# Attention and two quantised convolutions: phases of equal length on TensorE, and what is moved around them

## The chip, the cores and the metric

The kernel runs on one core of one Trainium2 chip. The metric is device time in microseconds (us), the median over executions. Engines are named as in the profile: PE (TensorE matmul), PEld (its weight loads), DVE (VectorE), ACT (ScalarE), POOL (GpSimd) and SP (SyncE, here a queue of DMAs).

## The reference, cut to what matters

```python
# layer 0, x: (4, 128, 64, 64); 4 heads of 32 channels, 4096 positions per image
x_norm = group_norm(x)                       # 8 groups of 16 channels
q, k, v = split(qkv_w @ x_norm + qkv_b)      # each to (b, head, position, 32)
attn = softmax(q @ k.T * 32**-0.5)           # 4096 x 4096 for each image and head
x = x + proj_w @ (attn @ v) + proj_b
# layer 1
out = relu(batchnorm(conv3x3(x, lsq_quantize(w1, alpha1))))
out = batchnorm(conv3x3(out, lsq_quantize(w2, alpha2)))
return relu(out + x)
```

`lsq_quantize` rounds w / alpha to 3 bits. The batch norms take their statistics over all four images, so no image can finish layer 1 alone.

## The kernel before, in words

**Tiles.** An image has 4096 positions: 8 chunks of 512 for queries (`qb`, 0 to 7), 32 tiles of 128 for keys (`kt`, 0 to 31). A block is one image and one `qb`; there are 32, numbered `n`. A step is one block and one `kt`: 1024 steps. The scores of a step are two pairs of heads. For each pair `scores` (L425) issues four matmuls into one of three PSUM tiles `s`, and ACT (L427) writes the exponentials into half of a tile `p` (128 x 4 heads x 512, 1 MB). There are eight such tiles, in `ppool`; the first two to be handed out are the halves of image 0's x, which stay until its last projection. `weights` (L438) multiplies all four heads of `p` with v into `acc`, 512 columns a head; an f32 matmul appears as two instructions in the trace. Scores run in row groups of 64 (64*128 in the trace), products with v and projections in column groups of 32 (128*32).

**Sums of the softmax.** DVE adds each `p` to `r` (L450, first of them L448). For the steps in `MOVED` (six of 32) POOL issues a DMA instead that adds `p` to `rm` (L445, first L443), and in the next block `merge` (L471) adds `rm` to `r`. A `p` is free when the product and the add, or the move, are done.

**Order.** It is written out by hand. PE runs phases: three pairs of scores, the product of one step, three pairs, the products of two steps, and so on:

```python
for s, w in ((3, 1), (3, 2)):
    run_scores(s)
    run_weights(w)
```

After each product `side` runs what `schedule` has listed for that `kt`. Matmuls beside the attention are put at `slots`, the ends of the one-step phases. A "visit" is a projection in two column halves (L301: "pk", "pq", "pv" for k, q, v of a chunk; L467: "l", the row sums) followed, a step later, by its evacuation: for k and q an ACT activation (L335) and a DVE instruction (L336), then a POOL DMA to DRAM (`kd`, `qd`); for v a DVE add (L355); for the sums an ACT copy `ls` (L475). A visit's two halves go to one place or to two. Visits share two PSUM banks (`psa`) with `acc`. Block n + 1 also finishes block n: the sums, their inversion by way of DRAM (`spread`, `invert`, `gather`), `weigh` on DVE (L514, "av"), `project` (L301, "po") and `store` (L524, L525 "y"). `acc` is copied by ACT (L460, "av") at a block's end.

**Image to image.** While image b runs, image b + 1's norm (`norm_parts`, with POOL, DVE and three small matmul groups) and projections are visited. Image 0 projects some chunks before the loop and the others in blocks 0 and 1, with x from the pinned halves. In the last image DVE quantises both weights piece by piece (`taps`, L174 to L191) into `wq`. SP issues all loads in order: x (L230), k (L394), v (L398), q (L405).

**After attention.** Two convolutions in bands of 16 rows (`load_band` L558, `split_band` L549 and L550, 36 matmuls each half at L722), each with batch statistics and a copy into `cv`. `mid` is an SBUF pool that opens where the attention's pools have closed.

Of the kernel before, what the change touches and what calls it, by code (L numbers as in the profile page):

```python
# [16 lines left out]
F32 = mybir.dt.float32  # L17
# [61 lines left out]
def _fast_body(ctx, tc, x, norm_w, norm_b, qkv_wt, qkv_b, proj_wt, proj_b,  # L79
# [56 lines left out]

    wq = [const.tile([P, TAPS, P], F32R, name=f"wq{i}") for i in range(2)]
    alpha_s = []  # L140
    gfac = 1.0 / math.sqrt(float(P * P * TAPS) * QP)

    def quant_tasks(pool):

        tasks = []
        for i, (w, alpha) in enumerate(((w1, alpha1), (w2, alpha2))):
# [20 lines left out]
            for c in range(3):  # L167


                def taps(i=i, c=c, w=w, t=t):  # L170
                    tk, tq = (pool.tile([P, 2, FB], F32, name=f"t{n}{i}{c}", tag=n) for n in "kq")
                    wr, q0, qh, ql = (u[:, e, : 3 * P].rearrange("p (t o) -> p t o", o=P)
                                      for u in (tk, tq) for e in range(2))
                    nc.sync.dma_start(out=wr, in_=w[:, 3 * c : 3 * c + 3, :])  # L174
                    yield
                    nc.vector.tensor_scalar(q0, wr, t["inv"], -8.0, ALU.mult, ALU.max)
                    nc.vector.tensor_scalar(q0, q0, 8.0, None, ALU.min)
                    nc.vector.tensor_scalar(qh, q0, SPLIT, None, ALU.add)
                    yield
                    nc.vector.tensor_scalar(qh, qh, SPLIT, None, ALU.subtract)  # L180
                    nc.vector.tensor_tensor(ql, q0, qh, ALU.subtract)
                    nc.vector.scalar_tensor_tensor(wr, qh, t["a_h"], wr, ALU.mult, ALU.subtract)
                    yield
                    nc.vector.scalar_tensor_tensor(wr, qh, t["a_l"], wr, ALU.mult, ALU.add)
                    nc.vector.scalar_tensor_tensor(wr, ql, t["a_h"], wr, ALU.mult, ALU.add)
                    nc.vector.scalar_tensor_tensor(wr, ql, t["a_l"], wr, ALU.mult, ALU.add)
                    yield
                    nc.vector.scalar_tensor_tensor(q0, wr, t["ninv"], q0, ALU.mult, ALU.add)
                    nc.vector.tensor_scalar(q0, q0, QN, QP, ALU.max, ALU.min)
                    nc.vector.tensor_scalar(q0, q0, ROUND, None, ALU.add)  # L190
                    nc.vector.tensor_scalar(wq[i][:, 3 * c : 3 * c + 3, :], q0, ROUND, None,  # L191
                                            ALU.subtract)

                tasks.append(taps)
        return tasks
# [3 lines left out]

    dram = ctx.enter_context(tc.tile_pool(name="dram", bufs=1, space=bass.MemoryType.DRAM))
    kpool = ctx.enter_context(tc.tile_pool(name="kpool", bufs=NB + 1))
    pss = ctx.enter_context(tc.tile_pool(name="pss", bufs=3, space=PSUM))
    psa = ctx.enter_context(tc.tile_pool(name="psa", bufs=2, space=PSUM))
# [5 lines left out]
    qpool = att.enter_context(tc.tile_pool(name="qpool", bufs=2))  # L211
    stage = att.enter_context(tc.tile_pool(name="stage", bufs=1))
    xpool = att.enter_context(tc.tile_pool(name="xpool", bufs=3))
    ppool = att.enter_context(tc.tile_pool(name="ppool", bufs=8))
    rpool = att.enter_context(tc.tile_pool(name="rpool", bufs=1))
    sums = att.enter_context(tc.tile_pool(name="sums", bufs=2))
    wpool = att.enter_context(tc.tile_pool(name="wpool", bufs=1))
# [189 lines left out]

    blocks = [(b, qb) for b in range(B) for qb in range(NB)]
    pts, acc, rsum, msum = {}, {}, {}, {}
    MOVED = (4, 9, 14, 19, 24, 28)  # L410


    def scores(pair):
# [14 lines left out]

    def weights(step):
        n, kt = divmod(step, NK)
        v = vs[blocks[n][0], kt // KB]
        pt = pts[step]
        if kt == 0:
            acc[n] = psa.tile([P, FB], F32, name=f"acc{n}", tag="a")
        for h in range(HEADS):
            nc.tensor.matmul(acc[n][h * D : (h + 1) * D, :], v[:, kt % KB, h * D : (h + 1) * D],  # L438
                             pt[:, h, :], start=(kt == 0), stop=(kt == NK - 1))
        if kt in MOVED:  # L440
            if kt == MOVED[0]:
                msum[n] = rpool.tile([P, HEADS, FB], F32, name=f"rm{n}", tag="rm")
                nc.gpsimd.dma_start(out=msum[n], in_=pt)  # L443
            else:
                nc.gpsimd.dma_start(out=msum[n], in_=pt, accum_op=ALU.add)  # L445
# [132 lines left out]
        load_k(b, j)  # L578
        load_v(b, j)

    for what, j in (("k", 0), ("q", 0), ("k", 1), ("v", 0), ("k", 2), ("v", 1), ("k", 3), ("v", 2)):
        for f in first_chunk(j, what, True):
            f()
        if what == "v":
            load_k(0, j + 1)


# [3 lines left out]
    def fetch(b, j):  # L591
        xin[b, j] = load_x(b, j)

    def schedule(n, before):
        b, qb = blocks[n]
        todo = []
        slots = [kt for kt in range(NK - 1) if (n * NK + kt) % 3 == 0]
        two = b + 1 < B and qb in (2, 3)
        full = two or n == 1

        def add(kt, f):
            todo.append((kt, f))

        def visit(kts, first, second, evacuate=None):
            add(kts[0], first)
            add(kts[-1], second)
            if evacuate:
                add(kts[-1] + 1, evacuate)

        if before:  # L610
            add(1, before["merge"])
            kts = slots[3:4] if full else slots[3:5]
            visit(kts, lambda: before["sums"](0), lambda: before["sums"](1))
            kt = kts[-1]
            add(kt + 1, before["spread"])
            add(kt + 3, before["invert"])
            add(kt + 4, before["gather"])
            add(kt + 6, before["residual"])
            add(slots[9] - 2, before["weigh"])
            add(slots[9], before["project"])  # L620
            add(slots[9] + 1, before["store"])
        if n + 1 < len(blocks):
            add(14, lambda: load_q(*blocks[n + 1]))
        if n == 0:
            for kt, what, j in ((0, "k", 4), (2, "q", 1), (3, "v", 3), (6, "k", 5), (9, "k", 6),
                                (12, "v", 4), (15, "k", 7), (18, "v", 5), (21, "v", 6),
                                (24, "v", 7)):
                visit((kt,), *first_chunk(j, what, False))
                if what == "k":
                    add(kt + 2, lambda j=j: load_k(0, j))  # L630
        if n == 1:
            for i, j in zip((0, 1, 2, 4, 5, 6), range(2, NB)):
                visit(slots[i : i + 1], *first_chunk(j, "q", False))
        if b + 1 < B:
            if qb == 1:
# [4 lines left out]
                late[b] = norm_parts(b + 1, st)  # L640
                add(15, late[b][0])
                for i in (0, 1):
                    add(slots[7 + i], late[b][1 + 2 * i])
                    add(slots[7 + i] + 1, late[b][2 + 2 * i])
            if qb == 2:
                add(slots[0], late[b][5])
                add(slots[0] + 1, late[b][6])
            chunks = {1: (), 2: (0, 1), 3: (2, 3), 4: (4,), 5: (5,), 6: (6,), 7: (7,)}
            for i, j in enumerate(chunks.get(qb, ())):
                p = project_parts(b + 1, j, lambda j=j: xin[b + 1, j])  # L650
                if not two:
                    places = dict(k=slots[0:2], q=slots[5:7], v=slots[7:9])
                elif i == 0:
                    places = dict(k=slots[1:2], q=slots[2:3], v=slots[4:5])
                else:
                    places = dict(k=slots[5:6], q=slots[6:7], v=slots[7:9])
                    add(8, lambda j=j: fetch(b + 1, j))
                for what, kts in places.items():
                    visit(kts, *p[what])
            if qb > 0 and qb + 1 in chunks:  # L660
# [15 lines left out]

    pieces = (piece for task in quant_tasks(stage) for piece in task())
    steps = len(blocks) * NK
    at = {"pair": 0, "step": 0}
    todo, parts = [], {}  # L680

    def side(kt):
        while todo and todo[0][0] <= kt:
            todo.pop(0)[1]()

    def run_scores(count):
# [2 lines left out]
            at["pair"] += 1  # L689

    def run_weights(count):
        for _ in range(min(count, steps - at["step"])):
            n, kt = divmod(at["step"], NK)
            if kt == 0:
                assert not todo
                todo[:] = schedule(n, parts.get(n - 1))
            weights(at["step"])
            at["step"] += 1
            if kt == NK - 2:
                parts[n] = finish_parts(n)  # L700
            if kt == NK - 1:
                parts[n]["copy"]()
            else:
                side(kt)

    run_scores(2)
    while at["step"] < steps:
        for s, w in ((3, 1), (3, 2)):
            run_scores(s)
            run_weights(w)  # L710

# [30 lines left out]

    mid = ctx.enter_context(tc.tile_pool(name="mid", bufs=1))
    cv = [mid.tile([P, N], F32, name=f"cv{b}") for b in range(B)]

    def batch_norm(i, st):

# [38 lines left out]
    def first(m):  # L788
        if m == 5:
            count_bad()  # L790
        if m + 3 < len(bandlist):
            load_band(*bandlist[m + 3])
        if m + 2 < len(bandlist) and m > 0:
# [512 lines left out]
```

## Time and profile before

| | |
|---|---|
| median of 3 executions | 2590.27 us (2589.32 to 2590.64) |
| the profiled execution, its time | 2589.98 us |
| the profiled execution, its span | 2588.2 us |
| granted PE clock | 0.992 |
| attention loop in the trace | about 29 to 2266 us |
| convolutions | about 2266 us to the end |

The span is from the first to the last instruction in the trace. A row of a group gives its busy time and the mean length of one instruction, then the engine's idle time before the group and what ended most of it. A row of the timeline gives the start, the length, the engine and line, and how many like instructions are merged (x12 at L425 is three pairs of scores).

### The profile page before, as it was taken

Reading aid. Unit: us, or ns where it says so; the run is one execution under the profiler, and the core shown is the slowest. Engines: PE = TensorE matmul, PEld = TensorE weight load, DVE = VectorE, ACT = ScalarE, POOL = GpSimd, SP = SyncE. Lnnn points to the kernel's source line nnn. Section 1 sums busy time; section 2 is a strip of 40 time slices with the busy share of each in tenths; the row PEclk is TensorE's granted clock in tenths of the full one; section 3 lists DMA queues with packets and bytes.
Section 4 is the critical chain, followed back from the end, with each engine's and each line's share of the span. In section 5 each row is a group of like instructions: output and inputs, shape, how many; then the busy total and the mean of one; then the engine's idle time right before and its main releaser. Section 6 shows DMA issues by size and latency. Waiting matters only on the chain.

```text
span 2588.2 us, 48399 instructions
## 1 busy us (share of the span) xinstructions
PE 2517.2 (97%) x20394; PEld 1223.4 (47%) x20394; DVE 2140.3 (83%) x1402; ACT 2081.9 (80%) x2275; POOL 281.4 (11%) x456
## 2 busy tenths in 40 slices
PE   6999999999999999999999999999999999999894
PEld 3444444444444444444444444444444444477773
DVE  5898888888988898888988988888999998953344
ACT  4888899999988999999988899999889898911223
POOL 2111111111011111110011111110000000100000
PEclk9999999999999999999999999999999999999997
DMA  5876766698667767697667666986655757634004
GB/s 160 191 187 172 177 161 149 154 206 201 162 148 178 178 155 171 149 225 171 160 171 161 164 159 150 207 202 142 151 130 126 154 126 148 146 80 145 1 1 164
DMA packets 147417, 400.04 MB, mean 155 GB/s; under 512 B 59240, under 2 KB 60008, under 8 KB 118648
## 3 DMA queue, kind: packets, MB, share of 16 engines
q0 software_dynamic: 45888, 280.59, 47.9%
q1 hardware_dynamic: 100728, 115.23, 16.8%
q8 instruction: 162, 2.65, 0.4%
q10 hardware_dynamic: 576, 1.05, 0.1%
q14 instruction: 63, 0.52, 0.1%
HBM read 105.32 MB, written 55.83 MB: 62 GB/s over the span
## 4 chain that ended last, share of the span: by engine, by line
PE 88%; DVE 5%; issue 3%; DMA 2%; ACT 1%; POOL 0%; SPq 0%; DVEq 0%; POOLq 0%; ACTq 0%
PE s L425 39%; PE acc L438 34%; PE c L722 9%; DVE r L450 3%; DMA rm<-p 2%; PE l L467 1%; PE po L301 1%; PE pk L301 1%; PE pq L301 1%; PE pv L301 1%; ACT p L427 1%; DVE res L844 1%; DMA xh<-in_x_dram 0%; DMA q<-qst 0%; DVE st L570 0%
## 5 line engine op out<-in xcount | busy, mean ns | idle before, releaser
L427 ACT ACTIVATE p<-s 128x1024 f32<-128x1024 f32 x2048 | 1940.2, 1034 | 235.0 <-PE s L425 158.7
L450 DVE TENSOR_TENSOR r<-r,p 128x2048 f32<-128x2048 f32 x768 | 1758.4, 2290 | 97.3 <-ACT p L427 48.1
L425 PE MATMUL s<-q,k 64*128 64x512 f32 x8192 | 1162.3, 413 | 3.9 <-ACT p L427 2.2
L438 PE MATMUL acc<-p,v 128*32 128x512 f32 x8192 | 1021.1, 601 | 0.6 <-DVE v L355 0.6
L425 PEld LDWEIGHTS s<-q,k 64*128 64x128 f32 x8192 | 711.7, 185 | 631.9 <-issue 298.0
L438 PEld LDWEIGHTS acc<-p,v 128*32 128x32 f32 x8192 | 198.6, 109 | 453.7 <-issue 446.3
L445 POOL DMA_DIRECT2D rm<-p x160 | 138.6, 866 | 950.7 <-ACT p L427 783.6
L775 ACT COPY cv<-c 128x512 f32<-128x512 f32 x64 | 37.6, 587 | 220.8 <-DVE st L774 220.8
L722 PE MATMUL c<-hi,wq 128*128 128x512 f32 x576 | 150.1, 405 | 8.3 <-DVE hi L805 6.8
L722 PE MATMUL c<-lo,wq 128*128 128x512 f32 x576 | 148.1, 402 | 0.0
L774 DVE BATCH_NORM_STATS2 st<-c 128x6 f32<-128x512 f32 x64 | 44.7, 699 | 124.5 <-PE c L722 102.5
L722 PEld LDWEIGHTS c<-hi,wq 128*128 128x128 f32 x576 | 109.4, 191 | 40.1 <-issue 8.9
L722 PEld LDWEIGHTS c<-lo,wq 128*128 128x128 f32 x576 | 109.0, 189 | 28.9
L448 DVE TENSOR_TENSOR r<-p,p 128x2048 f32<-128x2048 f32 x32 | 73.3, 2291 | 25.0 <-ACT p L427 25.0
L336 DVE SCALAR_TENSOR_TENSOR kst<-pk,b,kst 128x512 fp32r<-128x512 f32 x32 | 24.0, 751 | 73.2 <-ACT kst L335 73.2
L336 DVE SCALAR_TENSOR_TENSOR qst<-pq,b,qst 128x512 fp32r<-128x512 f32 x32 | 24.0, 750 | 41.6 <-ACT qst L335 41.6
L471 POOL DMA_DIRECT2D r<-rm x31 | 26.3, 848 | 159.8 <-PE s L425 91.9
L340 POOL DMA_DIRECT2D qd<-qst x31 | 23.3, 753 | 177.6 <-DVE qst L336 130.2
L443 POOL DMA_DIRECT2D rm<-p x32 | 17.8, 556 | 223.3 <-ACT p L427 136.4
L335 ACT ACTIVATE kst<-pk,b 128x512 fp32r<-128x512 f32 x32 | 22.4, 701 | 21.7 <-PE pk L301 21.7
L340 POOL DMA_DIRECT2D kd<-kst x28 | 20.6, 734 | 167.6 <-DVE kst L336 159.6
L467 PE MATMUL l<-r,ones 128*32 128x256 f32 (+1 forms) x504 | 37.9, 383 | 0.5 <-issue 0.5
(129 smaller groups left out, 672.0 us busy)
## 6 DMA issues: line engine op xcount, KB each, us to landing
rm<-p POOLq DMA_DIRECT2D x192, 1024.0 KB, 7.9
q<-qd SPq DMA_DIRECT2D x248, 128.0 KB
r<-rm POOLq DMA_DIRECT2D x31, 1024.0 KB, 7.1
x<-in_x_dram SPq DMA_DIRECT2D x80, 256.0 KB
k<-kd SPq DMA_DIRECT2D x124, 128.0 KB
qd<-qst POOLq DMA_DIRECT2D x31, 512.0 KB, 6.9
kd<-kst POOLq DMA_DIRECT2D x28, 512.0 KB, 4.0
y<-x POOLq DMA_DIRECT2D x32, 256.0 KB, 5.0
```

The costliest lines, as they stand in the source:

```text
L301: nc.tensor.matmul(out[cs, :], w[:, cs], x, start=True, stop=True)
L336: nc.vector.scalar_tensor_tensor(lo, ps[what], bias, t[:, 0, :], ALU.add, ALU.subtract)
L340: (nc.sync if start else nc.gpsimd).dma_start(out=dst[b, j].rearrange("s p n -> p s n"), in_=t)
L425: nc.tensor.matmul(s[:, i, :], k[r, half, c0 : c0 + P], q[r, half, part, :], start=(part == 0), stop=(part == 1))
L427: nc.scalar.activation(pts[step][:, 2 * half : 2 * half + 2, :], s, AF.Exp, scale=SCALE)
L438: nc.tensor.matmul(acc[n][h * D : (h + 1) * D, :], v[:, kt % KB, h * D : (h + 1) * D], pt[:, h, :], start=(kt == 0), stop=(kt == NK - 1))
L445: nc.gpsimd.dma_start(out=msum[n], in_=pt, accum_op=ALU.add)
L448: nc.vector.tensor_tensor(rsum[n], pts[step - 1], pt, ALU.add)
L450: nc.vector.tensor_tensor(rsum[n], rsum[n], pt, ALU.add)
L467: nc.tensor.matmul(t["l"][h * D : (h + 1) * D, cs], ones, r[:, h, cs], start=first, stop=end)
L722: nc.tensor.matmul(ps[:, j, :].rearrange("p (r w) -> p r w", w=W), w[:, tap, :], part[:, j * RB + kh : j * RB + kh + RB, kw : kw + W], sta ...
L774: nc.vector.bn_stats(st[:, b * NB + c, :], ps[:, j, :])
```

## The change

It rewrites the order in the attention loop and moves a few buffers:

- The product of a step is cut into two halves of 256 columns. PE alternates three pairs of scores with three halves, and the loop begins with three pairs in place of two. Visits stand at the last half of such a phase (`ends`), and `schedule` counts in halves; the places of the visits are new.
- `ppool` has nine tiles in place of eight. In the last image's blocks 1 to 6 seven steps in place of six are moved by DMA.
- The second convolution's weights are quantised into a tile that POOL stores to DRAM (`wqd`). After attention SP loads them (`raw_w`), and DVE copies them into `wq[1]` in the first convolution.
- The second image's norm and projections come one block later. Of image 0, v's chunk 3 is projected before the loop, q's chunk 1 later in block 0, and q's chunks 2 to 7 in block 1 take x from DRAM again.

```diff
-    ppool = att.enter_context(tc.tile_pool(name="ppool", bufs=8))
+    ppool = att.enter_context(tc.tile_pool(name="ppool", bufs=9))
...
+    MOVED, MOVED_LAST = (4, 9, 14, 19, 24, 28), (3, 7, 11, 15, 19, 23, 27)
...
-    def weights(step):
+    def weights(step, half):
...
+        cs = slice(half * FB // 2, (half + 1) * FB // 2)
         for h in range(HEADS):
-            nc.tensor.matmul(acc[n][h * D : (h + 1) * D, :], v[:, kt % KB, h * D : (h + 1) * D],
-                             pt[:, h, :], start=(kt == 0), stop=(kt == NK - 1))
+            nc.tensor.matmul(acc[n][h * D : (h + 1) * D, cs], v[:, kt % KB, h * D : (h + 1) * D],
+                             pt[:, h, cs], start=(kt == 0 and half == 0),
+                             stop=(kt == NK - 1 and half == 1))
+        if half == 0:
+            return
...
-        slots = [kt for kt in range(NK - 1) if (n * NK + kt) % 3 == 0]
-        two = b + 1 < B and qb in (2, 3)
+        ends = [p for p in range(2 * NK - 2) if (2 * n * NK + p) % 3 == 2]
+        two = b + 1 < B and qb in ((3, 4, 5) if b == 0 else (2, 3))
...
+        def visit(i, first, second, evacuate=None, split=True):
+            at_half(ends[i], first)
+            e = ends[i + 1 if split else i]
+            at_half(e, second)
             if evacuate:
-                add(kts[-1] + 1, evacuate)
+                at_half(e + 1, evacuate)
...
+            e = visit(5 if two else 4 if n == 1 else 6, lambda: before["sums"](0), lambda: before["sums"](1),
+                      split=not two and n != 1)
...
+            at_half(ends[18] - 4, before["weigh"])
+            at_half(ends[18], before["project"])
+            at_half(ends[18] + 2, before["store"])
         if n + 1 < len(blocks):
-            add(14, lambda: load_q(*blocks[n + 1]))
+            add(24 if n == 0 else 14, lambda: load_q(*blocks[n + 1]))
         if n == 0:
...
+            for i, what, j in ((0, "k", 4), (2, "k", 5), (4, "v", 4), (6, "k", 6), (8, "v", 5),
+                               (10, "k", 7), (12, "q", 1), (14, "v", 6), (16, "v", 7)):
+                visit(i, *first_chunk(j, what, False), split=False)
...
         if n == 1:
...
+            for i, j in zip((0, 2, 8, 10, 12, 14), range(2, NB)):
+                if j > 3:
+                    at_half(ends[i - 3], lambda j=j: fetch(0, j))
+                visit(i, *project_parts(0, j, lambda j=j: xin[0, j])["q"], split=False)
...
                 if not two:
-                    places = dict(k=slots[0:2], q=slots[5:7], v=slots[7:9])
...
+                    for what, i in dict(k=1, q=10, v=13).items():
+                        visit(i, *p[what])
+                    continue
+                for what, e in (dict(k=2, q=7, v=9) if i == 0 else dict(k=11, q=13, v=15)).items():
+                    visit(e, *p[what], split=False)
...
-    run_scores(2)
-    while at["step"] < steps:
-        for s, w in ((3, 1), (3, 2)):
-            run_scores(s)
-            run_weights(w)
+    run_scores(3)
+    while at["half"] < 2 * steps:
+        run_scores(3)
+        run_weights(3)
...
+    raw_w = mid.tile([P, TAPS, P], F32, name="raw_w")
+    wq.append(mid.tile([P, TAPS, P], F32R, name="wq1"))
+    nc.sync.dma_start(out=raw_w, in_=wqd)
...
+        if m == 6:
+            nc.vector.tensor_copy(wq[1], raw_w)
```

More of the change, by code (lines that the diff above doesn't have):

```diff
@@ L135, in rsqrt_eps @@
         return r
-    wq = [const.tile([P, TAPS, P], F32R, name=f"wq{i}") for i in range(2)]
+    dram = ctx.enter_context(tc.tile_pool(name="dram", bufs=1, space=bass.MemoryType.DRAM))
+    wq = [const.tile([P, TAPS, P], F32R, name="wq0")]
+    wqd = dram.tile([P, TAPS, P], F32, name="wqd")
     alpha_s = []
@@ L190, in taps @@
                     nc.vector.tensor_scalar(q0, q0, ROUND, None, ALU.add)
-                    nc.vector.tensor_scalar(wq[i][:, 3 * c : 3 * c + 3, :], q0, ROUND, None,
-                                            ALU.subtract)
+                    cs = slice(3 * c, 3 * c + 3)
+                    if i == 0:
+                        nc.vector.tensor_scalar(wq[0][:, cs, :], q0, ROUND, None, ALU.subtract)
+                    else:
+                        nc.vector.tensor_scalar(ql, q0, ROUND, None, ALU.subtract)
+                        nc.gpsimd.dma_start(out=wqd[:, cs, :], in_=ql)
                 tasks.append(taps)
         return tasks
-    dram = ctx.enter_context(tc.tile_pool(name="dram", bufs=1, space=bass.MemoryType.DRAM))
     kpool = ctx.enter_context(tc.tile_pool(name="kpool", bufs=NB + 1))
@@ L409, in _fast_body, with moved @@
     pts, acc, rsum, msum = {}, {}, {}, {}
-    MOVED = (4, 9, 14, 19, 24, 28)
+    MOVED, MOVED_LAST = (4, 9, 14, 19, 24, 28), (3, 7, 11, 15, 19, 23, 27)
+    def moved(n):
+        b, qb = blocks[n]
+        return MOVED_LAST if b == B - 1 and 0 < qb < NB - 1 else MOVED
     def scores(pair):
@@ L434, in weights @@
         pt = pts[step]
-        if kt == 0:
+        if kt == 0 and half == 0:
             acc[n] = psa.tile([P, FB], F32, name=f"acc{n}", tag="a")
+        cs = slice(half * FB // 2, (half + 1) * FB // 2)
         for h in range(HEADS):
-            nc.tensor.matmul(acc[n][h * D : (h + 1) * D, :], v[:, kt % KB, h * D : (h + 1) * D],
-                             pt[:, h, :], start=(kt == 0), stop=(kt == NK - 1))
-        if kt in MOVED:
-            if kt == MOVED[0]:
+            nc.tensor.matmul(acc[n][h * D : (h + 1) * D, cs], v[:, kt % KB, h * D : (h + 1) * D],
[3 more added lines that the diff above has]
+            return
+        if kt in moved(n):
+            if kt == moved(n)[0]:
                 msum[n] = rpool.tile([P, HEADS, FB], F32, name=f"rm{n}", tag="rm")
@@ L579, in load_kv @@
         load_v(b, j)
-    for what, j in (("k", 0), ("q", 0), ("k", 1), ("v", 0), ("k", 2), ("v", 1), ("k", 3), ("v", 2)):
+    for what, j in (("k", 0), ("q", 0), ("k", 1), ("v", 0), ("k", 2), ("v", 1), ("k", 3), ("v", 2),
+                    ("v", 3)):
         for f in first_chunk(j, what, True):
             f()
-        if what == "v":
+        if what == "v" and j < 3:
             load_k(0, j + 1)
@@ L596, in schedule, with at_half @@
         todo = []
-        slots = [kt for kt in range(NK - 1) if (n * NK + kt) % 3 == 0]
-        two = b + 1 < B and qb in (2, 3)
-        full = two or n == 1
+        ends = [p for p in range(2 * NK - 2) if (2 * n * NK + p) % 3 == 2]
+        two = b + 1 < B and qb in ((3, 4, 5) if b == 0 else (2, 3))
+        def at_half(p, f):
+            todo.append((p, f))
         def add(kt, f):
[L602 to L606, printed above, removed]
+            todo.append((2 * kt + 1, f))
@@ L607, in visit @@
+        def visit(i, first, second, evacuate=None, split=True):
+            at_half(ends[i], first)
+            e = ends[i + 1 if split else i]
+            at_half(e, second)
             if evacuate:
-                add(kts[-1] + 1, evacuate)
+                at_half(e + 1, evacuate)
+            return e
         if before:
             add(1, before["merge"])
-            kts = slots[3:4] if full else slots[3:5]
-            visit(kts, lambda: before["sums"](0), lambda: before["sums"](1))
@@ L614, in schedule @@
[L614 to L621, printed above, removed]
+            e = visit(5 if two else 4 if n == 1 else 6, lambda: before["sums"](0), lambda: before["sums"](1),
+                      split=not two and n != 1)
@@ L622, in schedule @@
+            at_half(e + 2, before["spread"])
+            at_half(e + 6, before["invert"])
+            at_half(e + 8, before["gather"])
+            at_half(e + 12, before["residual"])
+            at_half(ends[18] - 4, before["weigh"])
+            at_half(ends[18], before["project"])
+            at_half(ends[18] + 2, before["store"])
         if n + 1 < len(blocks):
-            add(14, lambda: load_q(*blocks[n + 1]))
+            add(24 if n == 0 else 14, lambda: load_q(*blocks[n + 1]))
         if n == 0:
[L625 to L628, printed above, removed]
+            for i, what, j in ((0, "k", 4), (2, "k", 5), (4, "v", 4), (6, "k", 6), (8, "v", 5),
+                               (10, "k", 7), (12, "q", 1), (14, "v", 6), (16, "v", 7)):
+                visit(i, *first_chunk(j, what, False), split=False)
@@ L629, in schedule @@
                 if what == "k":
-                    add(kt + 2, lambda j=j: load_k(0, j))
+                    at_half(ends[i] + 5, lambda j=j: load_k(0, j))
+        if n == 0:
+            for j in (2, 3):
+                add(25 + j, lambda j=j: fetch(0, j))
         if n == 1:
-            for i, j in zip((0, 1, 2, 4, 5, 6), range(2, NB)):
-                visit(slots[i : i + 1], *first_chunk(j, "q", False))
+            for i, j in zip((0, 2, 8, 10, 12, 14), range(2, NB)):
+                if j > 3:
+                    at_half(ends[i - 3], lambda j=j: fetch(0, j))
+                visit(i, *project_parts(0, j, lambda j=j: xin[0, j])["q"], split=False)
@@ L634, in schedule @@
+        qn = qb if b else qb - 1
         if b + 1 < B:
-            if qb == 1:
+            if qn == 1:
                 st = small.tile([P, NB, 6], F32, name=f"st{b + 1}", tag="st")
@@ L642, in schedule @@
                 for i in (0, 1):
[L643 to L648, printed above, removed]
+                    at_half(ends[13 + 2 * i], late[b][1 + 2 * i])
+                    at_half(ends[13 + 2 * i] + 3, late[b][2 + 2 * i])
+            if qn == 2:
+                at_half(ends[0], late[b][5])
+                at_half(ends[0] + 1, late[b][6])
+            if b == 0:
+                chunks = {2: (), 3: (0, 1), 4: (2, 3), 5: (4, 5), 6: (6,), 7: (7,)}
+            else:
+                chunks = {1: (), 2: (0, 1), 3: (2, 3), 4: (4,), 5: (5,), 6: (6,), 7: (7,)}
             for i, j in enumerate(chunks.get(qb, ())):
@@ L651, in schedule @@
                 if not two:
-                    places = dict(k=slots[0:2], q=slots[5:7], v=slots[7:9])
[L653 to L656, printed above, removed]
+                    for what, i in dict(k=1, q=10, v=13).items():
[3 more added lines that the diff above has]
+                    visit(e, *p[what], split=False)
+                if i == 1:
                     add(8, lambda j=j: fetch(b + 1, j))
-                for what, kts in places.items():
-                    visit(kts, *p[what])
-            if qb > 0 and qb + 1 in chunks:
+            if qn > 0 and qb + 1 in chunks:
                 add(22, lambda j=chunks[qb + 1][0]: fetch(b + 1, j))
@@ L678, in _fast_body, with side @@
     steps = len(blocks) * NK
-    at = {"pair": 0, "step": 0}
+    at = {"pair": 0, "half": 0}
     todo, parts = [], {}
-    def side(kt):
-        while todo and todo[0][0] <= kt:
+    def side(p):
+        while todo and todo[0][0] <= p:
             todo.pop(0)[1]()
@@ L691, in run_weights @@
     def run_weights(count):
-        for _ in range(min(count, steps - at["step"])):
-            n, kt = divmod(at["step"], NK)
-            if kt == 0:
+        for _ in range(min(count, 2 * steps - at["half"])):
+            n, p = divmod(at["half"], 2 * NK)
+            if p == 0:
                 assert not todo
                 todo[:] = schedule(n, parts.get(n - 1))
-            weights(at["step"])
-            at["step"] += 1
-            if kt == NK - 2:
+            weights(*divmod(at["half"], 2))
+            at["half"] += 1
+            if p == 2 * NK - 3:
                 parts[n] = finish_parts(n)
-            if kt == NK - 1:
+            if p == 2 * NK - 1:
                 parts[n]["copy"]()
             else:
-                side(kt)
-    run_scores(2)
-    while at["step"] < steps:
-        for s, w in ((3, 1), (3, 2)):
-            run_scores(s)
-            run_weights(w)
+                side(p)
+    run_scores(3)
+    while at["half"] < 2 * steps:
+        run_scores(3)
+        run_weights(3)
     bandlist = [(b, g) for b in range(B) for g in range(H // BR)]
```

## The prediction

> **What bounds the kernel now.** I began with the page: busy shares, the span in slices, the costliest groups.
>
> ```profile
> PE 2517.2 (97%) x20394; PEld 1223.4 (47%) x20394; DVE 2140.3 (83%) x1402; ACT 2081.9 (80%) x2275; POOL 281.4 (11%) x456
> ...
> L427 ACT ACTIVATE p<-s 128x1024 f32<-128x1024 f32 x2048 | 1940.2, 1034 | 235.0 <-PE s L425 158.7
> L450 DVE TENSOR_TENSOR r<-r,p 128x2048 f32<-128x2048 f32 x768 | 1758.4, 2290 | 97.3 <-ACT p L427 48.1
> L425 PE MATMUL s<-q,k 64*128 64x512 f32 x8192 | 1162.3, 413 | 3.9 <-ACT p L427 2.2
> L438 PE MATMUL acc<-p,v 128*32 128x512 f32 x8192 | 1021.1, 601 | 0.6 <-DVE v L355 0.6
> ```
>
> TensorE (PE) is the bound: 97%, with almost no idle time put down to its two large groups. But a group's busy time also holds waits between its own matmuls, so I read PE's timeline, where the distance from one start to the next is the true price. Around 260 us (columns: start, length, engine, line), and then ACT beside it:
>
> ```profile
> 260.02 1.66 PE L425 MATMUL s<-q,k 64*128 64x512 f32 x12
> 261.61 1.07 PE L438 MATMUL acc<-p,v 128*32 128x512 f32 x8
> 262.61 1.89 PE L425 MATMUL s<-q,k 64*128 64x512 f32 x12
> 264.43 1.92 PE L438 MATMUL acc<-p,v 128*32 128x512 f32 x16
> 266.28 1.67 PE L425 MATMUL s<-q,k 64*128 64x512 f32 x12
> 267.88 1.07 PE L438 MATMUL acc<-p,v 128*32 128x512 f32 x8
> 268.76 1.05 PE L301 MATMUL pk<-x,wn 128*32 128x256 f32 x16
> ```
>
> ```profile
> 260.16 0.59 ACT L460 COPY av<-acc 128x512 f32<-128x512 f32 x1
> 260.85 5.61 ACT L427 ACTIVATE p<-s 128x1024 f32<-128x1024 f32 x6
> ```
>
> Three pairs of scores take 1.59 to 1.60 us (260.02 to 261.61), a product with v for one step 1.00 (261.61 to 262.61), for two steps 1.85. The short phase is thus 2.60 us, the long one 3.45. ACT needs 2.86 for three exponentials (half of 5.61, plus a seam). After a short phase with nothing beside it the next scores find the third PSUM buffer still full: 262.61 to 264.43 is 1.82, not 1.60. Over the whole timeline of PE, 683 score phases, I count some 118 of these, of 0.15 to 0.25 us: **20.6 us** hidden in "busy". The larger stops, read the same way: 5.5 at 37 to 50 us (a projection waits for its PSUM bank, 1.7 and 2.6, then scores 1.3), 3.4 at 85 to 175 (the largest, 1.8, is ACT waiting for a buffer that a move "rm<-p" holds), 5.9 at 1917 to 2057 (a projection waits for DVE's "av").
>
> [...] the product of one step takes 0.88 when a 128*32 projection follows (267.88 to 268.76), 1.00 when 64*128 scores do, so 0.12 a switch. [...]
>
> **The change, part by part.**
>
> 1. *Halves and equal phases.* Each step's 4 products of 512 columns become 8 of 256; phases become 3 pairs and 3 halves. The number of phases, hence of switches, stays at 683. Is the split free? No row has p times v at 256 columns. The nearest rows, same weights of 32 columns: a projection of two 256-column halves ("pk" x16) takes 0.98 before scores, "po" with 512 columns x8 takes 0.97, "pv" with four times 128 columns x32 takes 0.98. So below 0.01 per split. From above: 0.03 per split, the most by which a first group exceeds a following one (0.88 against 1.85-1.00=0.85), times 1024 is +31. [...] I take 0. Three halves: 1.85-0.85/2=1.425, so a phase of 1.60+1.42=**3.02 us** against ACT's 2.86: the short-phase stalls go, **-20.6**.
>
> 2. *What is late next: ACT's copies.* A copy of 0.59 to 0.70 ("av", "ls", "kst", "qst") comes behind three exponentials, begun 0.76 after a phase's start. They end at 3.62, the copy at 4.21 to 4.32, while the next exponential could start at 3.02+0.76=3.78: late by 0.43 to 0.54. A 2.60 phase with no delay costs 0.16, so the next stall is 0.16+(2.60-3.02)+0.43 or 0.54 = 0.17 or 0.28 if the delayed phase has no visit; with half a visit (0.43) it is nil. From the new places: k is exposed in 17 blocks (0.28), the sums in 23 (0.17), "av" in a third of 31 (0.17); q's delay meets v's visit. Sum 4.8+3.9+1.8=**+10.5**. If every one of about 112 copies stalled, it would be 25 to 31.
>
> 3. *Opening.* Visits of block 0 stand two phases apart, so the 5.5 goes. v's chunk 3 moves ahead of the loop (0.87), where scores wait for "q<-qst" to 31.92 in any case: its 0.98 in the loop is saved. **-6.5**. k 4 to 7 keep their POOL and SP issues, some earlier or later; "load_q" goes from step 14 to 24. Its own wait for "qd" (landing 4.3, POOL queue before it) and eight SP issues end some 5 us before block 1 needs it, by about 11 steps of 2.1 us less 20. Taken as 0; up to +5 if not.
>
> 4. *Nine buffers, x from DRAM, the norm later.* Six more loads of 256 KB on SP, in a stretch where the 16 DMA engines are 75% busy; the two pinned x buffers come free after block 0. Of the 3.4 I take **-2.5**.
>
> 5. *Seventh move in six blocks.* Six adds fewer, 6x2.29=13.7 us of DVE, which is 93% busy there (519.87 of 560 us). DVE is not the bound, only late at two projections: half of 5.9, **-3**. Moves then stand four steps apart, about 8.5 us, against 7.4 to land; POOL's queue behind them holds "y" and the merge, with slack of a block.
>
> 6. *Second weights.* Three POOL stores of 192 KB, in blocks with DMA at 65%: 0. At the end SP issues "raw_w" (590 KB) before band 3. At the 231 GB/s seen there, 2.6 us, less than one band's 8.6 us of convolution: between 0 and 3, taken **+1**. The DVE copy costs about 0.76 (the cast of 1188 columns) where DVE is 39% busy: 0.
>
> Unknown collisions in the rewritten order: **+2**. Sum: -20.6+10.5-6.5-2.5-3+1+2 = **-19** on a span of 2588.2. That execution took 2589.98, 0.3 below the median 2590.27, so about **2571**.
>
> **Rivals.**
>
> *A. The halves cost.* Each extra group of four costs 0.03 [...]: +31 on 2571 is 2602. For it: PEld's loads double and the first group after a switch is dearer. Against: the pk/po/pv rows. It decides from 19/1024=0.019 us per split: there the gain is gone. Chance 0.15.
>
> *B. ACT's copies take it back.* All 112 stall at 0.28: +31 instead of +10.5, so 2592 less what visits cover, about 2588. For it: ACT is 90% busy in mid-attention. Against: visits cover q and v by their places. Chance 0.14.
>
> *C. The phases equalise nothing,* since the third half waits for the current phase's first exponential. It ends about 0.76+0.95=1.7 after the start and is wanted at 1.60+0.85=2.45, 0.7 later, so unlikely: only parts 3 to 5 stay, 2590-12+3=2581. Chance 0.13.
>
> Forecast: 0.58, its own range 2558 to 2583.
>
> **How the numbers follow.** C and the forecast are faster, with a little of B: 0.73. B is mostly within 0.2%, about what a measurement of this kernel can tell: 0.10. A and the bad end of B: 0.17. For 8 in 10 the range runs from 2556 (no new stall at all) to 2600 (the split at 0.028 us).
>
> **What would show it.** In the new timeline three halves before scores at 1.42 to 1.44 us: right; 1.50 or more: A. Score phases of 1.60 after phases without a visit, and of 1.77 to 1.88 only behind a copy: step 2; a whole comb of them: B. ACT's idle time grows by a few us only. The stops at 37 to 50 us and at 173 gone, those near 1917 and 2055 halved. A first stop at block 1 ended by "q<-qd" would refute step 3. I am wrong if the time is above 2585.

## The result, and the profile after

The changed kernel takes 2589.36 us at the median, the kernel before 2590.53 in the same comparison: ratio 0.9995, interval 0.9983 to 1.0008. That is no change that can be measured; forecast were 2571 us. The profiled execution has a span of 2587.8 us against 2588.2. So the question is where 19 us of expected gain went. One execution of c_hold (below) took 5305.06 us, twice the others, and is left out of its ratio.

The page after, rows that answer to those of before:

```profile
PE 2504.4 (97%) x28586; PEld 1491.1 (58%) x28586; DVE 2125.1 (82%) x1397; ACT 2086.2 (81%) x2275; POOL 288.8 (11%) x465
...
L436 PE MATMUL s<-q,k 64*128 64x512 f32 x8192 | 1143.7, 410 | 9.8 <-ACT p L438 7.9
L450 PE MATMUL acc<-p,v 128*32 128x256 f32 x16384 | 1026.7, 383 | 1.0 <-DVE v L361 1.0
```

The scores are 18.6 us shorter in busy time (1162.3 before), the products 5.6 longer (1021.1), and PE as a whole 12.8 shorter, yet the span is the same. A busy time holds short waits too (in the kernel before, the row of scores at 262.61 us is 1.89 long, its neighbours 1.66 and 1.67), so the rows alone do not say where the time went. PE's timeline shows the equal phases as intended (start, length, engine, line, operation, count):

```profile
1006.32 1.50 PE L450 MATMUL acc<-p,v 128*32 128x256 f32 x24
1007.76 1.66 PE L436 MATMUL s<-q,k 64*128 64x512 f32 x12
1009.35 1.50 PE L450 MATMUL acc<-p,v 128*32 128x256 f32 x24
1010.78 1.66 PE L436 MATMUL s<-q,k 64*128 64x512 f32 x12
```

Three halves 1.43 us, three pairs 1.59: 3.02 a phase. I went through PE's whole timeline of both kernels, took the undisturbed length from every row and added up the rest; the choice of that length shifts such a sum by about 1 us. The comb of small stops (up to 0.3 us) fell from 21.6 to **1.4 us**. The larger stops rose from 20.9 to **34.8 us**:

| larger stops, us | before | after |
|---|---|---|
| opening, to 60 us | 8.7 | 3.4 |
| rest of blocks 0 and 1, to 230 us | 3.4 | 7.4 |
| 230 to 1700 us | 1.0 | 5.4 |
| last image, to 2260 us | 6.6 | 18.6 |
| tail | 1.2 | 0 |

The balance is -20.2 +13.9 = -6.3 us. Some 3 to 7 us go into the products (below); one or two stay unexplained. Three of the stops, as they look. First the end of block 7 at 607 us, a row of ACT, then one of PE:

```profile
608.33 1.94 ACT L438 ACTIVATE p<-s 128x1024 f32<-128x1024 f32 x2 [2.24 <-DMA rm<-p]
```

```profile
609.40 0.73 PE L436 MATMUL s<-q,k 64*128 64x512 f32 x4 [1.36 <-ACT p L438]
```

The bracket is the idle time and what ended it. ACT wants a tile p, a move still holds it, and PE is left without a free score bank. Second the largest stop, at 1907 us in the last image, in four views: SP's queue before and after, then DVE and PE after.

```profile
1851.65 5.11 SPq L405 DMA_DIRECT2D q<-qd  x8
...
1896.95 0.35 SPq L174 DMA_DIRECT2D tk<-in_L_conv_w_dram  x1
```

```profile
1887.97 12.94 SPq L411 DMA_DIRECT2D q<-qd  x8
...
1901.81 0.35 SPq L177 DMA_DIRECT2D tk<-in_L_conv_w_dram  x1
```

```profile
1910.56 0.42 DVE L179 TENSOR_SCALAR tk<-tk,inv 128x384 f32<-128x384 f32 x1 [10.62 <-DMA tk<-in_L_conv_w_dram]
```

```profile
1917.02 1.93 PE L307 MATMUL po<-av,wp 128*32 128x512 f32 x8 [8.70 <-DVE av L529]
```

Before, q's loads were out long before the weights' piece `tk`, and DVE began on that piece at 1906.43 without a wait. After, SP issues it only behind q's eight loads; DVE stands 10.6 us before it with its adds and "av" queued behind; PE waits for "av". Third, in block 1, the sums wait for the merge of rm into r (shown with d_open).

### The profile page after: what moved, and what is told of

Its sections match the earlier page's. It is cut to its first block, busy times and chain, and to the rows that moved or that the text cites. A ratio compares the mean times of both kernels' runs of the same rounds, so it can differ in the third digit from the quotient of the medians.

```text
span 2587.8 us, 64784 instructions
## 1 busy us (share of the span) xinstructions
PE 2504.4 (97%) x28586; PEld 1491.1 (58%) x28586; DVE 2125.1 (82%) x1397; ACT 2086.2 (81%) x2275; POOL 288.8 (11%) x465
## 4 chain that ended last, share of the span: by engine, by line
PE 87%; DMA 7%; issue 3%; DVE 2%; ACT 1%; POOL 0%; SPq 0%; POOLq 0%; ACTq 0%; DVEq 0%
PE s L436 38%; PE acc L450 34%; PE c L749 10%; DMA rm<-p 4%; PE po L307 1%; PE l L482 1%; PE pk L307 1%; PE pv L307 1%; PE pq L307 1%; ACT p L438 1%; DMA q<-qd 1%; DVE r L465 1%; DVE res L876 1%; DMA x<-in_x_dram 0%; DMA r<-rm 0%
## 5 line engine op out<-in xcount | busy, mean ns | idle before, releaser
L436 PE MATMUL s<-q,k 64*128 64x512 f32 x8192 | 1143.7, 410 | 9.8 <-ACT p L438 7.9
L450 PE MATMUL acc<-p,v 128*32 128x256 f32 x16384 | 1026.7, 383 | 1.0 <-DVE v L361 1.0
L450 PEld LDWEIGHTS acc<-p,v 128*32 128x32 f32 x16384 | 462.9, 109 | 486.0 <-issue 248.6
L460 POOL DMA_DIRECT2D rm<-p x166 | 144.3, 869 | 874.8 <-ACT p L438 522.8
L307 PE MATMUL po<-av,wp 128*32 128x512 f32 x256 | 35.2, 622 | 9.1 <-DVE av L529 9.1
L341 ACT ACTIVATE kst<-pk,b 128x512 fp32r<-128x512 f32 x32 | 22.4, 701 | 21.6 <-PE pk L307 21.6
```

The lines of the kernel that those rows point to most:

```text
L307: nc.tensor.matmul(out[cs, :], w[:, cs], x, start=True, stop=True)
L436: nc.tensor.matmul(s[:, i, :], k[r, half, c0 : c0 + P], q[r, half, part, :], start=(part == 0), stop=(part == 1))
L450: nc.tensor.matmul(acc[n][h * D : (h + 1) * D, cs], v[:, kt % KB, h * D : (h + 1) * D], pt[:, h, cs], start=(kt == 0 and half == 0), stop= ...
```

## The experiments

Each ratio is to the kernel before on the same chip, with its 95% interval. The runs named a_ (but a_uneven) and b_split share one chip, those named c_ and a_uneven a second, those named d_ a third, so runs of two groups are compared through their ratios. Line numbers of the same statement differ a little from run to run, since an edit adds lines.

### Is it the split?

b_split is the kernel before, with

```diff
-        for h in range(HEADS):
+        for half, h in ((i, h) for i in range(2) for h in range(HEADS)):
+            cs = slice(half * FB // 2, (half + 1) * FB // 2)
...
```

and with the matmuls' output and p cut to the columns `cs`.

> The kernel before with each step's product issued as two halves of 256 columns, one right after the other, and nothing else changed (phases stay one step and two steps). The phase lengths of the two traces (2.85 us for three steps in the kernel before, 2 x 1.43 in the changed one; with a visit 2.73 against 2.75) say 0.01 to 0.02 us for each three splits, 341 of these: +3 to +7 us, 2593 to 2597 us. Rival S, that the split eats the whole comb of 20 us: 2608 to 2612 us.

Measured: 1.0006 (0.9997 to 1.0015), 2593.88 us against 2592.24. The split costs 0 to 4 us, not 20: rival S falls. Its trace says the same by another way: a product of two steps takes 1.86 us (from 1003.29 to 1005.15) against 1.85 (from 1001.99 to 1003.84 in the kernel before), 0.01 for two steps or some 5 us over 1024.

### The equal phases undone

a_uneven is the changed kernel with

```diff
-        run_scores(3)
-        run_weights(3)
+        for w in (2, 4):
+            run_scores(3)
+            run_weights(w)
```

and the visits at those phases' ends.

> The changed kernel with phases of two and four halves in turn, as before, instead of three and three (places of visits at the ends of these phases). Undoes the equal phases alone. If the comb of 0.15 to 0.25 us stops is due to the short phase, it is back: some 230 of the 341 short phases have no visit, +35 us at 0.16, less what the longer ones give back to moves and DVE: 2605 to 2625 us. Rival: the comb's saving was never real time, because PE would have waited elsewhere; then 2588 to 2593 us, with less waiting for moves.

Measured: 1.0135 (1.0118 to 1.0152), 2624.73 us, at the upper end of what the comb said. Its timeline of PE has the long score phase (1.76) behind the short product:

```profile
1002.73 1.07 PE L450 MATMUL acc<-p,v 128*32 128x256 f32 x16
1003.73 1.83 PE L436 MATMUL s<-q,k 64*128 64x512 f32 x12
1005.49 1.93 PE L450 MATMUL acc<-p,v 128*32 128x256 f32 x32
```

So the equal phases are worth their time in this order of visits; the rest of the change took it back.

### Seven moves, and q's place in SP's queue

a_moves6:

```diff
-    MOVED, MOVED_LAST = (4, 9, 14, 19, 24, 28), (3, 7, 11, 15, 19, 23, 27)
+    MOVED, MOVED_LAST = (4, 9, 14, 19, 24, 28), (4, 9, 14, 19, 24, 28)
```

> The changed kernel with six moved steps in place of seven in blocks 1 to 6 of the last image. Theory M (moves): the seventh move puts the moves 4 steps, about 8.5 us, apart while one takes 7.6 us at the median and up to 13.8 to land; so POOL waits for the move before, p tiles stay held, ACT waits for them and PE stops at about 1984, 2137 and 2187 us. Then these three go (about 5 us), POOL's waits of rm for rm in the last image fall from 161 us towards the 44 of the kernel before, and the time is 2581 to 2585 us. Theory Q (order on SP): the last image's largest stop, 8.9 us at 1907 us, comes from weights that SP loads late behind q, and moves matter little: 2588 to 2590 us. Rival S (the split costs what the comb gave): 2588 to 2590 us.

Measured: 0.9978 (0.9968 to 0.9988), some 4 us under the changed kernel's 0.9995, whose interval it just meets. Between 1700 and 2260 us a move on POOL waits for the move before it (rm for rm) 46.8 us in 7 waits, against 148.0 in 18; the 161 of the expectation has two waits of the merge in it. The stop at 1984 us shrinks from 2.4 to 0.8, those at 2137 and 2187 are gone. PE in the changed kernel, then in a_moves6:

```profile
2187.41 1.19 PE L436 MATMUL s<-q,k 64*128 64x512 f32 x8
2190.49 0.73 PE L436 MATMUL s<-q,k 64*128 64x512 f32 x4 [1.89 <-ACT p L438]
```

```profile
2186.97 1.66 PE L436 MATMUL s<-q,k 64*128 64x512 f32 x12
```

Theory M holds for these three stops. But DVE has its seventh add back, and PE now waits 3.7 us for "av" at 2050, so that the last image's larger stops fall only from 18.6 to some 17 us in the trace. By the times, the add that the seventh move saved was worth less than the tile that it held.

a_loadq, and a_both with both edits:

```diff
-            add(24 if n == 0 else 14, lambda: load_q(*blocks[n + 1]))
+            add(24 if n == 0 else 14 if n == 1 else 2, lambda: load_q(*blocks[n + 1]))
```

> The changed kernel with the load of the next block's q listed at step 2 instead of step 14 from block 2 on, so that SP issues it before the spread and the gather of the sums and not behind them. Theory Q: the quantised weights' load is issued at once, DVE no longer waits 10.6 us for it, the stop of 8.9 us at 1907 us and its two after-effects (0.9 and 0.75 us) go: 2578 to 2581 us. Theory M: the stop stays, since p tiles are held by the moves: 2588 to 2590 us. Rival S: no change.

> The changed kernel with both edits: six moved steps everywhere and q's load at step 2. If M and Q are both right and add up, 10 + 5 us: 2572 to 2576 us. If only Q is right 2578 to 2581, if only M 2581 to 2585; rival S 2588 to 2590 us.

Measured: a_loadq 0.9997 (0.9983 to 1.001), a_both 0.9981 (0.9972 to 0.999): no gain of its own, and both forecasts missed. The trace of a_loadq (2598.68 us, one of its slowest executions, against a median of 2592.9) has lost the 8.9 us at 1907, but has new stops at block starts, 3.3 at 1176, 3.2 at 1734 and 5.0 at 2038 us. That of a_both (2585.51 us) has lost it too, and has 3.1 each at 1172 and 1731. My reading, which these runs do not test by themselves, is that q's 1 MB now lands where the moves are late. As a test of Q by time they were inconclusive, since they mend one lateness in the place of another. I then asked why moves are late at all where there are only six.

### Stores ahead of moves in POOL's queue

POOL's queue at the same block's end, before and after:

```profile
579.92 0.85 POOL L445 DMA_DIRECT2D rm<-p  x1 [9.49 <-ACT p L427]
587.75 0.75 POOL L340 DMA_DIRECT2D qd<-qst  x1 [6.98 <-DMA rm<-p]
591.04 0.86 POOL L445 DMA_DIRECT2D rm<-p  x1 [2.53 <-ACT p L427]
600.67 0.58 POOL L359 DMA_DIRECT2D vd<-vst  x1 [8.77 <-DVE vst L355]
602.93 0.83 POOL L445 DMA_DIRECT2D rm<-p  x1 [1.68 <-ACT p L427]
```

```profile
580.63 0.75 POOL L346 DMA_DIRECT2D qd<-qst  x1 [9.70 <-DVE qst L342]
581.37 0.91 POOL L460 DMA_DIRECT2D rm<-p  x1
588.22 0.58 POOL L365 DMA_DIRECT2D vd<-vst  x1 [5.94 <-DVE vst L361]
596.34 0.84 POOL L460 DMA_DIRECT2D rm<-p  x1 [7.55 <-DMA rm<-p]
608.74 0.83 POOL L460 DMA_DIRECT2D rm<-p  x1 [11.55 <-issue]
```

Before, a move waits for ACT's p and goes; the store of q comes behind it, and the one store ahead of a move, v's at 600.67, is done before that move's p is. After, the visits of q and v end a little earlier in the block, their stores stand ahead of the moves of steps 19 and 24, and POOL waits there for DVE. The first store is issued after a wait of 9.70 us, and "rm<-p" at 581.37 goes out only 0.7 us behind it, though it had no need of that store and the move before it had landed at 578.8 (570.09 and 8.7 us). The moves then run into each other until the block ends: this one lands only at 595.82, after 14.4 us, the next, issued at 596.34, at 608.22, and with that ACT has its tile (the stop at 607 above).

c_hold, on top of a_moves6, keeps the stores in a list that is emptied behind the next move:

```diff
+            elif b > 0:
+                held.append(lambda: nc.gpsimd.dma_start(out=dst[b, j].rearrange("s p n -> p s n"), in_=t))
...
+            while held:
+                held.pop(0)()
```

> Six moves everywhere, as in a_moves6 (0.9978 of the kernel before), and each store of a next image's k, q or v ("kd", "qd", "vd") is issued on POOL behind the next move instead of at its evacuation. Theory P (order on POOL): in the changed kernel the visits of q and v end a little before steps 19 and 24, so POOL's queue has their stores, which wait for DVE, ahead of the moves of those steps; the moves slip, those of steps 24 and 28 meet the loads of the next image's k and v at a block's end, and ACT waits for p tiles there. Then the stops near 607, 618, 1165 and 1725 us go, some 5 to 6 us: ratio about 0.9957, 2580 us on a chip where the kernel before takes 2591. Rival D (DVE is what is late, the moves only suffer from it): no change from a_moves6, 0.9978.

Measured: **0.9957** (0.9941 to 0.9973), the number expected, though its interval still meets that of a_moves6. Waits of POOL in a_moves6, on which it is built, and in c_hold (total us, times, longest):

```profile
POOL rm L460 <- ACT p L438: 595.6, 78, 13.4
POOL qd L346 <- DVE qst L342: 255.5, 28, 16.6
POOL rm L460 <- DMA rm<-p: 193.1, 32, 11.7
```

```profile
POOL rm L463 <- ACT p L441: 908.1, 113, 12.6
POOL rm L463 <- DMA rm<-p: 189.2, 24, 12.5
...
POOL qd L349 <- DVE qst L343: 57.5, 7, 16.6
```

Waiting for ACT's p is the good wait: the move goes out as soon as its data is there, 113 times as in the kernel before. The waits of one move for another are as long as in a_moves6 (189.2 against 193.1), but they no longer reach ACT, whose waits for moves fall from 8.5 to 1.0 us. The stops at 607, 618 and 1725 us are gone, that of 1165 remains at 0.9. Theory P holds, and rival D (DVE late on its own) falls: no add was taken off DVE.

### "av" earlier

c_weigh, on top of a_moves6, and c_holdweigh with both edits:

```diff
-            at_half(ends[18] - 4, before["weigh"])
+            at_half(ends[18] - 10, before["weigh"])
```

> Six moves everywhere, and the multiplication "av" by the inverted sums is listed ten halves ahead of the projection "po" instead of four, so that it stands earlier in DVE's order. Theory W: three stops of a_moves6 in the last image (5.6 at 1908, 0.8 at 1984, 3.7 at 2050 us, with after-effects of 0.9 and 1.3) are PE waiting for that one instruction behind DVE's adds; they go or shrink, 6 to 10 us: ratio 0.9940 to 0.9955. Rival D: DVE, 93% busy with the weights' pieces, stays as late and p tiles are held instead: the stops change their place, ratio about 0.9978.

> Six moves everywhere with both edits (stores behind the moves, "av" ten halves ahead). P and W both right: 0.992 to 0.9935, about 2572 us where the kernel before takes 2591. Rival D: 0.9978.

Measured: c_weigh 0.9961 (0.9946 to 0.9975), a little short of what W said and not clear of a_moves6; c_holdweigh 0.9935 (0.9919 to 0.9952), at its weak end. PE's waits for "av" shrink (5.6 to 1.0 at 1908 us, 3.7 to 1.3 at 2050), but in part they become stops of 1.5 to 2.1 us a few phases on: in c_weigh DVE still stands 6.0 us for the weights' piece. W is half right: the instruction's place set who waited, not that DVE was late.

### The queue on SP, the places in block 1, the ninth buffer

Three edits on c_holdweigh: d_loadq (`8 if b == B - 1` for q's load), d_open, d_p8 (eight tiles p), and d_all with the first two.

```diff
-            e = visit(5 if two else 4 if n == 1 else 6, lambda: before["sums"](0), lambda: before["sums"](1),
+            e = visit(5 if two or n == 1 else 6, lambda: before["sums"](0), lambda: before["sums"](1),
-            for i, j in zip((0, 2, 8, 10, 12, 14), range(2, NB)):
+            for i, j in zip((1, 3, 8, 10, 12, 14), range(2, NB)):
```

> c_holdweigh (0.9935 of the kernel before) with q's load of the last image's blocks at step 8 instead of 14, ahead of the spread and the gather on SP. Theory Q (order on SP): DVE still waits 6.1 us for a piece of the weights near 1890 to 1905 us, because SP has its load behind q's eight; the stops from 1900 to 1920 us (1.0, 2.0, 0.7, 0.9) go: ratio 0.9915 to 0.992. Rival: a_loadq alone showed no gain, because q's loads, put at a block's start, met the moves there; if they still do, new stops at block starts in the last image and 0.9935 to 0.996.

> c_holdweigh with three places of block 1 changed: q's chunks 2 and 3 at phase ends 1 and 3 instead of 0 and 2, the sums of block 0 at 5 instead of 4. Theory O (places): the stops at 109 us (1.2, the projection waits for ACT's copy "av" to free a PSUM bank), 124 us (2.6, the sums wait for the merge of rm into r) and 129 us (1.2, its after-effect) are these two visits coming too early; they go, 4 to 5 us: ratio 0.9915 to 0.992. Rival: the merge is late by more than a phase (3.5 us), and the stop only moves: 0.993 to 0.994.

> c_holdweigh with both edits. If Q and O are right and add up, 9 us: ratio 0.990, about 2565 us where the kernel before takes 2591. If only one is right, 0.9915 to 0.992; if none, 0.9935.

> c_holdweigh with eight tiles of exponentials in place of nine. If the ninth is what lets moves be late without a stop (the equal phases keep half a step more in flight than before), ACT waits for moves at block ends again and the time rises by 5 to 15 us: ratio 0.9955 to 0.999. Rival: with the moves in order eight would do, and it is 0.993 to 0.994.

Measured: d_loadq 0.9913 (0.9896 to 0.993), d_open 0.9911 (0.9894 to 0.9927), d_all **0.9895** (0.9878 to 0.9911), d_p8 0.9973 (0.9963 to 0.9984). The first two overlap c_holdweigh's interval, and their traces carry them; d_all does not overlap it. In d_loadq DVE waits for the weights' piece no more than this, and of the stops from 1900 to 1920 us none is left:

```profile
1896.41 0.42 DVE L179 TENSOR_SCALAR tk<-tk,inv 128x384 f32<-128x384 f32 x1 [0.58 <-DMA tk<-in_L_conv_w_dram]
```

So Q was right about this stop. d_loadq differs from a_loadq in two ways, the moves in order and q's load moved in the last image only, to step 8 instead of 2; which of them made the gain show in the time is not separated. In block 1, PE and then POOL in c_holdweigh:

```profile
127.80 1.41 PE L487 MATMUL l<-r,ones 128*32 128x256 f32 x16 [2.37 <-DMA r<-rm]
```

```profile
117.67 0.75 POOL L349 DMA_DIRECT2D qd<-qst  x1 [16.60 <-DVE qst L343]
118.41 0.90 POOL L491 DMA_DIRECT2D r<-rm  x1
```

and in d_open:

```profile
126.24 1.05 PE L487 MATMUL l<-r,ones 128*32 128x256 f32 x16
```

```profile
110.75 0.84 POOL L491 DMA_DIRECT2D r<-rm  x1 [10.45 <-DMA rm<-p]
```

The sums follow the product at once, and the stops at 109 and 129 us are gone too. The two rows of POOL show why the merge was late: it is once more a store of q, waiting 16.6 us for DVE, that stood ahead of it (the list of c_hold holds only the stores of later images). With q's visit one phase on, the store comes behind the merge, which goes out 7.7 us earlier. No run tells what the later place of the sums adds to that.

d_p8 is slower than c_holdweigh, with intervals apart: in its trace, of its fastest execution (2579.73 us, median 2584.47), ACT waits for moves 12.2 us instead of 1.1, so this order needs the ninth buffer.

d_all, at 2565.64 us where the kernel before takes 2591.43, beats both kernels, and it keeps the equal phases of the change.

## Why the prediction was wrong, point by point

The saving that was forecast came, less a few us for the split. What failed is the price of the moved order: steps 4 and 5, the later blocks in step 3, and the unknown collisions. Steps 4 and 5 and the collisions were put at -3.5 us together; the stops that they stand for rose by 20.4 (3.4 to 7.4, 1.0 to 5.4 and 6.6 to 18.6 in the table).

- **Step 1, right.** Phases are 3.02 us as worked out, and the comb went from 21.6 to 1.4 us. The split was taken at 0; the rows give 2.86 for two phases of halves against 2.85 for one and two steps, and 2.75 against 2.73 with a visit, which is 3 to 7 us over 341 pairs of phases; b_split says 0 to 4. Rival A, 31, falls.
- **Step 2, mis-sized.** ACT's copies were to take back 10.5 us. They take part of 1.4. The changed kernel's ACT, with the copy of k:

```profile
1034.50 2.86 ACT L438 ACTIVATE p<-s 128x1024 f32<-128x1024 f32 x3 [0.65 <-ACT p L438]
1037.23 0.70 ACT L341 ACTIVATE kst<-pk,b 128x512 fp32r<-128x512 f32 x1
1037.80 5.63 ACT L438 ACTIVATE p<-s 128x1024 f32<-128x1024 f32 x6
```

From start to start the three exponentials take 2.73 and the copy 0.57, where I had used the lengths 2.86 and 0.70; each overlaps the next instruction by 0.13. The scores of that phase begin at 1036.71, so the next exponential could begin 0.76 later, at about 1037.48, and is late by 0.32, not 0.54. The stall is then 0.16-0.42+0.32=0.06; the scores of the phase after it, at 1039.74, take 1.66 instead of 1.59. Rival B falls with it: its 2588 us is the figure nearest to the measured time, but by luck.

- **Step 3, right for the opening** (8.7 to 3.4, and v's chunk hidden), and block 1 was not held up by q: the last of the eight loads was issued at 97.92 us, the first scores of block 1, by count, began at 104.59. (The sum for this margin was off: 11 steps of 2.1 us less 20 are 3, not 5.) But it followed "load_q" in block 0 only; the later blocks have no term in the sum and no reason for that. There the number 14 stayed while the places of the sums moved. In the block of the largest stop SP had issued q's loads at 1851.65, 37 us ahead of the sums' transfers; in the changed kernel they come at 1887.97, behind spread and gather, and the weights' piece behind them: 8.9 us, and 1.7 in the two stops after it. This is the largest single loss, in a place where the prediction's own sign was that the stops near 1917 and 2055 would be halved.
- **Step 4, wrong sign.** Of 3.4 us I took 2.5 off. The stop by a held p went, but the stops there grew to 7.4 us. Some 5 of them come from block 1: q's first visit now asks for a PSUM bank before "av" is copied out of it, and its store stands ahead of the merge on POOL (d_open takes 4.3 off).
- **Step 5, wrong sign.** "About 8.5 us, against 7.4 to land" was the failing comparison, of a spacing with a middle value: in the last image the moves take 7.6 us at the median and up to 13.8 to land, and the slack that was counted was that of "y" and the merge, not that of p. A tile that is moved is wanted again by ACT about six steps, some 13 us, later (my estimate: nine tiles, some three of them for scores ahead of the products, steps of 2.1 us). It was to gain 3 us; taking it back gained some 4.
- **Step 6, right:** one stop of 0.5 us in band 3, and from the first convolution on the two traces are 322.3 us each.
- **"Unknown collisions: +2", mis-sized.** In the middle of the kernel alone they cost 5.4 us (1.0 before), most of it from the order of stores and moves on POOL (c_hold leaves some 2). I had the rule of counting each queue that a step is moved past, and applied it to the k chunks of block 0, not to q and v in all others.
- **Rival C** falls too: it expected 2581 us because the phases would not equalise, and they did (a_uneven).

The gain was not lost in the place of the change. It was given back in three queues, POOL, SP and DVE, in which something short and urgent had come to stand behind something that waits or takes long: a move behind a store that waited 9.70 us, the weights' piece behind 12.94 us of q's loads, "av" behind DVE's wait of 10.62 us.

## What to carry to other kernels

When a hand-written order is shifted, list for each queue that issues DMAs what stands ahead of each urgent entry before and after; a place that kept its number can have changed its neighbours. A transfer that holds a buffer of a ring should be issued as soon as its data is there, and be compared with the ring by its longest landing, not its median (13.8 us against 7.6 in the last image). Work out how late an engine will be from the spacing of starts in the timeline, not from the lengths of instructions (0.57 us against 0.70 for the copy of k).

## What the runs showed that I had not expected

Cutting 1024 steps of four products of 512 columns into halves of 256, and so doubling PE's instructions there and its weight loads (each 8192 before, 16384 after), costs only a few us in 2590 (0 to 4 by the times, about 5 by the rows). And removing about 20 us of stops from PE, with DVE's and ACT's work nearly unchanged (busy 2140.3 and 2081.9 us before, 2125.1 and 2086.2 after), left a time that could not be told from the old one until five places in the orders of POOL, SP, DVE and PE were put right; each of these was worth some 4 to 7 us, and together they gave 26.
